# LSTM with a binary FFN on one core: x Wx computed in column tiles of 32 instead of on the whole array, and the activation tiles moved by 320 bytes

## The chip, the cores and the metric

The kernel runs on one core of one Trainium2 chip. The metric is the device time of one launch in microseconds: 328.22 us before, the median of three runs (328.02 to 329.63). A profile of one further execution shows what each engine did.

## The reference

The input x holds 32 sequences of 64 steps with 256 features. An LSTM with 256 hidden units runs over the steps and starts from `cond`; its hidden states go through an FFN of three layers whose weights are +1 or -1, given as booleans, and the result is added to x. All of it is float32.

```python
xW = x @ Wx + b                             # 32 x 64 x 1024, Wx is 256 x 1024
for t in range(64):
    a = xW[:, t] + prev_h @ Wh              # 32 x 1024
    i, f, o = sigmoid(a[:, :256]), sigmoid(a[:, 256:512]), sigmoid(a[:, 512:768])
    g = tanh(a[:, 768:])
    c = f * c + i * g
    h = o * tanh(c)
# FFN over all h: 512 (as [h, -h]) -> 1024 -> 1024 -> 256
y = s0 * ([h, -h] @ w(k0)); y = 2 * relu(y)
y = s1 * (y @ w(k1));       y = 2 * relu(y)
return x + s2 * (y @ w(k2))                 # w(k) = where(k, 1, -1)
```

## The kernel before

The 64 steps are cut into NB = 4 blocks of SB = 16. For a block of 16 steps and 32 sequences, x Wx is 512 columns wide, and so is each FFN matmul.

**x Wx** (`x_block`, L223 to L244). The 1024 outputs are cut into NM = 8 pieces of 128 rows (tile px, one PSUM bank each). Each piece is the product of 128x128 slices of Wx with the transposed x (tile xT, made by `turn_x`, L202, on VectorE), in two halves of 256 columns and with two slices of the contraction (k). The two float32 operands make every `nc.tensor.matmul` into two matmul instructions of the PE, so a piece has 4 matmuls and 8 instructions, and the kernel has 256 px instructions in all. A finished piece is moved by `finish_x` (L246): ScalarE adds the bias (tile xb, L254) and VectorE transposes it into xg (L251), where the 4 x 32 rows of the piece come to lie beside each other for the recurrence.

The order of Wx's columns in a piece isn't the order of the input. Row q*32 + j of a piece is output column q*64 + b*32 + j of the gate. So `order_wx` (L211) copies the columns of each gate g (tiles wx, wx_rest) into a tile wxo that has them in this order, two copies for each gate: the first on VectorE (L448), the others on ScalarE (L451, L459, L460).

**The recurrence.** `gates_from_h` (L284) computes h Wh of one step. The 32 sequences make the stationary side 32 columns wide, so four products with different quarters of Wh (q = 0 to 3) go to the four column tiles of 32 of the array: 8 matmuls, 16 instructions. `cell_step` (L298) adds xg on VectorE (tile `a`), takes sigmoid and tanh on ScalarE (sig, cand, th), forms kept, new, c and h on VectorE, and transposes h into hist, which the next step's gates read.

**The FFN** (`ffn_block`, L384) takes a block of h, split in two parts (hhi and hlo, made by `split_h`, L337 and L338), through the three layers: 128x128 weights, 512 columns, type float32r, one instruction for each matmul: 768 in all (L390, L419, L404).

**The order of the work.** Each engine executes its instructions in the order in which the program issues them. `x_block(0)` comes first and whole; then, for each step t, the gates of t, the cell's work, and then a share of the remaining matmuls, taken from a generator `fill()` that runs through x blocks 1 to 3 and then through the four FFN blocks. Steps 0 to 16 carry the three x blocks (10 or 12 px instructions a step, `goal`, L504), the later ones FFN matmuls (12 a step). What is left of the FFN after step 63 follows as a tail. `vector_queue` and `scalar_queue` hold the work that follows a piece until it has its turn in the step.

**The start.** Before its first real matmul, the PE multiplies zeros WARM_UP = 8 times (p_idle, L446). The loads go out on the queues of SP and ScalarE: x of block 0, Wx's gate 0, then on SP gate 1 (wx), gates 2 and 3 together (wx_rest, in a buffer of the xg pool), Wh, x of block 1, and the booleans of the FFN. A load is issued once the load eight places ahead of it has landed. During `x_block(0)` a dictionary `then` (L458) places further work after the n-th xg transposition: the order_wx of gates 2 and 3, `turn_x(1, 0)` (n = 5) and `turn_x(1, 1)` (n = 7), which make xT of block 1, and the transposition of the first h (hT, n = 6).

**Memory.** The pool const holds all weights of the recurrence and the FFN (wh, w0, w1, w2) and, behind them, small tiles, among them `warm`, of which the kernel uses two columns. The other pools, with x, xg, the activations (act), hist, hhi, hlo and the cell's tiles, follow. In this kernel the const pool ends on a multiple of 512 bytes, and so each tile of 2 KB or more in the later pools and each 128-column slice of the weights starts on such a multiple.

Of the kernel before, what the change touches and what calls it, by code (L numbers as in the profile page):

```python
# [24 lines left out]
F32 = mybir.dt.float32  # L28
# [8 lines left out]
def lstm_ffn(ctx: ExitStack, tc: tile.TileContext, x, cond, wx_d, wh_d, b_d, k0_d, k1_d, k2_d, s0_d, s1_d, s2_d, out):  # L37
    nc = tc.nc
    P = 128
    N, T, D = x.shape  # L40
    H = cond.shape[1]
    G = 4 * H
    NQ = 4
# [4 lines left out]
    NM = G // P  # L48
# [3 lines left out]
    SH = 4  # L52
    PER_STEP = 12
    LAG = SB + 1
    WARM_UP = 8

    const = ctx.enter_context(tc.tile_pool(name="const", bufs=1))
    xpool = ctx.enter_context(tc.tile_pool(name="x", bufs=4))
    gpool = ctx.enter_context(tc.tile_pool(name="xg", bufs=NB))
# [9 lines left out]
    def act(shape, dtype, name):  # L69
        return apool.tile(shape, dtype, tag="act", name=name)  # L70
# [18 lines left out]
    w1 = const.tile([P, FC0, F1], F32R, name="w1")  # L89
    w2 = const.tile([P, 2, FC1, P], F32R, name="w2")  # L90

    warm = const.tile([P, 40], F32, name="warm")
    nc.vector.memset(warm, 0.0)
    idle = const.tile([P, 512], mybir.dt.bfloat16, name="idle")
    nc.vector.memset(idle, 0.0)

    wx_rows = wx_d.rearrange("(q b j) g -> q j b g", q=NQ, b=2)
    wx_first = [act([P, 2, H], F32, f"wx_{g}") for g in range(2)]
    wx_rest = gpool.tile([P, 2, 2 * H], F32, tag="xg", name="wx_rest")
    wxf = wx_first + [wx_rest[:, :, ts(g, H)] for g in range(2)]  # L100

    def rows(t, q):
        return t[q * 32 : (q + 1) * 32]

    load_x(0, 0, [nc.sync, nc.scalar])
    for q in range(NQ):
        engine = (nc.sync, nc.scalar)[q % 2]
        engine.dma_start(out=rows(wx_first[0], q), in_=wx_rows[q, :, :, :H])
    load_x(0, 1, [nc.sync, nc.scalar])

    nc.scalar.activation(warm[:, 1:2], warm[:, :1], AF.Sigmoid)
# [1 line left out]
    b_rows = b_d.rearrange("(g q b j) -> q g b j", g=4, q=NQ, b=2)  # L113
    for q in range(NQ):
        nc.gpsimd.dma_start(out=b_raw[q * 32 : q * 32 + NM], in_=b_rows[q])
    for q in range(NQ):
        nc.sync.dma_start(out=rows(wx_first[1], q), in_=wx_rows[q, :, :, ts(1, H)])
    for q in range(NQ):
        nc.sync.dma_start(out=rows(wx_rest, q), in_=wx_rows[q, :, :, 2 * H :])
    wh_rows = wh_d.rearrange("(q b j) g -> q j b g", q=NQ, b=2)  # L120
    for q in range(NQ):
        nc.sync.dma_start(out=rows(wh, q), in_=wh_rows[q])
    h_first = const.tile([P, HQ], F32, name="h_first")
# [11 lines left out]
    for i in range(2):  # L135
        t = act([P, 2, F0], U8, f"k0_{i}")
# [63 lines left out]
    xT = {}  # L200

    def turn_x(i, half):  # L202
        full = act([P, SB // 2, 2, N], F32, f"xT{i}_{half}")
        nc.vector.transpose(
            full.rearrange("p t b n -> p (t b n)"), xq[i, half].rearrange("p t j -> p (t j)")
        )
        xT[i, half] = full

    wx = []

    def order_wx(g, copy):  # L211

        t = act([P, 2, 2, P], F32, f"wxo{g}")
        for k in range(2):
            copy(  # L215
                t[:, k].rearrange("p b (q j) -> p b q j", q=NQ),
                wxf[g][:, k, :].rearrange("p (q b j) -> p b q j", q=NQ, b=2),
            )
        wx.append(t)

    xg = {}

    def x_block(i):  # L223
        xg[i] = gpool.tile([P, SB, G // NQ], F32, tag="xg", name=f"xg{i}")
        side = 2 if i == 0 else 1
        for m0 in range(0, NM, side):
            ps = [ps_f.tile([P, 2, SB // 2, N], F32, tag="pf", name=f"px{i}_{m0 + j}") for j in range(side)]
            for half in range(2):
                for j in range(side):
                    g, b = divmod(m0 + j, 2)  # L230
                    for k in range(2):
                        nc.tensor.matmul(  # L232
                            ps[j][:, half],
                            wx[g][:, k, b, :],
                            xT[i, half][:, :, k, :],
                            start=(k == 0),
                            stop=(k == 1),
                            skip_group_check=True,
                        )
                        if k == 0:  # L240
                            yield 2
                    if half:
                        finish_x(i, m0 + j, ps[j])
                    yield 2  # L244
# [199 lines left out]
    p_idle = ps_f.tile([P, TB], F32, tag="pf", name="p_idle")  # L444
    for n in range(WARM_UP):
        nc.tensor.matmul(p_idle, idle[:, :P], idle, start=True, stop=True)  # L446
    turn_x(0, 0)
    order_wx(0, nc.vector.tensor_copy)  # L448
    turn_x(0, 1)
    nc.vector.transpose(bias, b_raw)  # L450
    order_wx(1, nc.scalar.copy)  # L451
    for i in range(4):
        load_bits(i)
    hT = const.tile([P, 2, N], F32, name="hT_first")
    c = cell.tile([P, HQ], F32, tag="c", name="c_first")
    nc.vector.memset(c, 0.0)

    then = {  # L458
        1: lambda: order_wx(2, nc.scalar.copy),  # L459
        3: lambda: order_wx(3, nc.scalar.copy),  # L460
        5: lambda: turn_x(1, 0),
        6: lambda: nc.vector.transpose(hT, h_first.rearrange("p (b j) -> p b j", b=2)),
        7: lambda: turn_x(1, 1),
    }
    n = 0
    for _ in x_block(0):
        if vector_queue:
            flush_vector()
            n += 1
            if n in then:  # L470
                then[n]()


    def fill():
        for i in range(1, NB):
            yield from x_block(i)
        for b in range(NB):
            yield from ffn_block(b)
# [14 lines left out]
    for t in range(T):  # L493
        g = gates_from_h(t, hT)
        c, hT = cell_step(t, g, c)
# [54 lines left out]
```

## Time and profile before

| what | value |
|---|---|
| median of three runs | 328.22 us (328.02 to 329.63) |
| the profiled execution | 329.2 us, span 327.4 us |
| PE busy | 316.1 us, 97% of the span |
| VectorE (DVE) busy | 175.0 us, 53% |
| ScalarE (ACT) busy | 127.5 us, 39% |
| first px matmul, first gates matmul | at 5.59 us and 21.61 us |
| steps 0 to 16 (with x Wx) | from 21.61 us to 86.70 us |
| HBM read, written | 8.16 MB, 2.10 MB |

In the rows of the page and of the trace, PE is the matmul row of TensorE, L is the line of the kernel, and `out<-in` are the program's tiles. A group's row gives its busy time in us and the mean time of one in ns, then the idle time of the engine ahead of it and what ended that. A row in order of time begins with its start and its length in us; in brackets stand the engine's idle time before it and what ended it. Matmuls overlap, so a row's length isn't its share of the PE's time; the distance from one start to the next is.

### The profile page before, as it was taken

To read this page: it belongs to the slowest core of one execution; us is meant where nothing else is said; L and a number is where in the kernel's file an instruction comes from. 1 tells how busy PE (TensorE), PEld (TensorE's weight loads), DVE (VectorE), ACT (ScalarE), POOL (GpSimd) and SP (SyncE) were. 2 spreads that over 40 slices of the span, in tenths; PEclk is the share of its full clock that TensorE was granted. 3 is DMA by queue.
4 is the path that set the end of the run, shared out by engine and by line. 5 is a ranking of instruction groups with operands and counts; after the bars stand their busy time and mean duration, and the time that the engine had idled before them with its cause. 6 is when DMAs were issued, how large, how long until landed. Compare 5 with 4: busy or idle time off the path is not lost.

```text
span 327.4 us, 5478 instructions
## 1 busy us (share of the span) xinstructions
PE 316.1 (97%) x2056; PEld 217.2 (66%) x2056; DVE 175.0 (53%) x540; ACT 127.5 (39%) x330; POOL 9.0 (3%) x27
## 2 busy tenths in 40 slices
PE   7998999999999999999999999999999999999992
PEld 3876666667666666666666666666666666888881
DVE  3357766765685445446856454568564444811114
ACT  1534576666553523233523232335332322511111
POOL 6200000000000000000000000000000000000001
PEclk9999999999999999999999999999999999999997
DMA  6956000105100000000010300000110000130002
GB/s 141 218 147 140 3 19 16 34 16 124 24 2 1 2 0 0 2 2 1 0 34 8 91 0 2 0 3 0 32 34 0 2 1 2 48 80 3 0 0 64
DMA packets 30538, 10.62 MB, mean 32 GB/s; under 512 B 27944, under 2 KB 29992, under 8 KB 30512
## 3 DMA queue, kind: packets, MB, share of 16 engines
q1 hardware_dynamic: 27904, 9.58, 12.1%
q10 hardware_dynamic: 2336, 0.66, 0.9%
q8 instruction: 16, 0.26, 0.3%
q0 software_dynamic: 272, 0.04, 0.1%
q14 instruction: 10, 0.08, 0.1%
HBM read 8.16 MB, written 2.10 MB: 31 GB/s over the span
## 4 chain that ended last, share of the span: by engine, by line
PE 81%; DVE 6%; DMA 4%; ACT 3%; SPq 3%; issue 1%; ACTq 0%; DVEq 0%
PE p L419 38%; PE gates L288 18%; PE p L390 10%; PE po L404 9%; PE px L232 7%; DMA wh<-in_L_cond_Wh_dram 2%; DVE xg L251 1%; ACT xb L254 1%; DVE a L300 1%; SPq L138 1%; DMA wx<-in_L_cond_Wx_dram 1%; DVE w L182 1%; ACT th L317 1%; DMA x<-in_x_dram 1%; DMA k<-in_L_ffn_k_dram 1%
## 5 line engine op out<-in xcount | busy, mean ns | idle before, releaser
L288 PE MATMUL gates<-wh,hist 128*32 128x256 f32 x1008 | 67.5, 385 | 2.7 <-DVE hist L324 2.7
L232 PE MATMUL px<-xT,wxo 128*128 128x256 f32 x256 | 62.1, 396 | 0.7 <-DVE wxo L215 0.7
L305 ACT ACTIVATE sig<-a 128x192 f32<-128x192 f32 x64 | 23.3, 364 | 95.8 <-DVE a L300 95.8
L232 PEld LDWEIGHTS px<-xT,wxo 128*128 128x128 f32 x256 | 48.6, 195 | 14.9 <-issue 5.8
L300 DVE TENSOR_TENSOR a<-gates,xg 128x256 f32<-128x256 f32 x64 | 27.0, 422 | 56.5 <-PE gates L288 56.3
L288 PEld LDWEIGHTS gates<-wh,hist 128*32 128x32 f32 x1008 | 26.9, 109 | 35.6 <-issue 20.2
L317 ACT ACTIVATE th<-c 128x64 f32<-128x64 f32 x64 | 16.4, 257 | 35.7 <-DVE c L315 35.4
L319 DVE TENSOR_TENSOR h<-sig,th 128x64 f32<-128x64 f32 x64 | 14.4, 225 | 24.4 <-ACT th L317 24.4
L251 DVE STREAM_TRANSPOSE xg<-xb 128x512 f32<-128x512 f32 x32 | 22.2, 695 | 9.2 <-ACT xb L254 9.2
L390 PE MATMUL p<-hhi,w 128*128 128x512 f32 x64 | 26.1, 408 | 0.0
L390 PE MATMUL p<-hlo,w 128*128 128x512 f32 x64 | 25.2, 393 | 0.0
L254 ACT ACTIVATE xb<-px,small 128x512 f32<-128x512 f32 x32 | 21.6, 675 | 4.9 <-PE px L232 4.9
L311 DVE TENSOR_TENSOR kept<-sig,c 128x64 f32<-128x64 f32 x63 | 13.2, 209 | 8.3 <-ACT sig L305 8.3
L324 DVE STREAM_TRANSPOSE hist<-h 128x64 f32<-128x64 f32 x64 | 15.7, 246 | 2.2
L390 PEld LDWEIGHTS p<-hhi,w 128*128 128x128 f32 x64 | 12.0, 187 | 6.1 <-issue 3.3
L315 DVE TENSOR_TENSOR c<-kept,new 128x64 f32<-128x64 f32 x64 | 14.4, 225 | 2.2
L307 ACT ACTIVATE cand<-a 128x64 f32<-128x64 f32 x64 | 15.4, 240 | 0.0
L313 DVE TENSOR_TENSOR new<-sig,cand 128x64 f32<-128x64 f32 x64 | 14.0, 219 | 0.0
L419 PE MATMUL p<-a_2h,w 128*128 128x512 f32 x32 | 13.9, 434 | 0.0
L390 PEld LDWEIGHTS p<-hlo,w 128*128 128x128 f32 x64 | 12.0, 188 | 2.4
L419 PE MATMUL p<-a_6h,w 128*128 128x512 f32 x32 | 13.5, 423 | 0.0
L419 PE MATMUL p<-a_4h,w 128*128 128x512 f32 x32 | 13.2, 414 | 0.0
(122 smaller groups left out, 487.7 us busy)
## 6 DMA issues: line engine op xcount, KB each, us to landing
x<-in_x_dram SPq DMA_DIRECT2D x60, 64.0 KB, 2.3
out_dram<-o SPq DMA_DIRECT2D x28, 64.0 KB, 1.8
bits<-in_L_ffn_k_dram SPq DMA_DIRECT2D x10, 128.0 KB, 2.3
wh<-in_L_cond_Wh_dram SPq DMA_DIRECT2D x4, 256.0 KB, 6.4
wx_rest<-in_L_cond_Wx_dram SPq DMA_DIRECT2D x4, 128.0 KB, 3.3
k<-in_L_ffn_k_dram SPq DMA_DIRECT2D x8, 64.0 KB, 1.9
wx<-in_L_cond_Wx_dram SPq DMA_DIRECT2D x6, 64.0 KB, 2.8
x<-in_x_dram ACTq DMA_DIRECT2D x4, 64.0 KB, 2.6
```

Source lines behind the costliest of these rows:

```text
L232: nc.tensor.matmul(ps[j][:, half], wx[g][:, k, b, :], xT[i, half][:, :, k, :], start=(k == 0), stop=(k == 1), skip_group_check=True,)
L251: nc.vector.transpose(out_t[:, :, ts(m, 32)], tmp.rearrange("p (t n) -> p t n", n=N))
L254: nc.scalar.activation(tmp, p.rearrange("p h t n -> p (h t n)"), AF.Identity, bias=bias[:, m : m + 1])
L288: nc.tensor.matmul(g[q * N : (q + 1) * N], hT[:, k, :], wh_q[:, k, q], start=(k == 0), stop=(k == 1), skip_group_check=True,)
L300: nc.vector.tensor_tensor(a.rearrange("p g j -> p (g j)"), g.rearrange("p g j -> p (g j)"), xg[t // SB][:, t % SB, :], ALU.add)
L305: nc.scalar.activation(sig, a[:, 0:3, :], AF.Sigmoid)
L307: nc.scalar.activation(cand, a[:, 3, :], AF.Tanh)
L317: nc.scalar.activation(th, c, AF.Tanh)
L324: nc.vector.transpose(hT, h.rearrange("p (b j) -> p b j", b=2))
L390: nc.tensor.matmul(p, w0[:, k, ts(m, P)], a[:, k, :], start=(n == 0), stop=(n == 3))
L404: nc.tensor.matmul(po[m], w2[:, m, k], a1[k][n], start=(k == 0 and n == 0), stop=(k == FC1 - 1 and n == 1))
L419: nc.tensor.matmul(p1[m], w1[:, k, ts(m, P)], a0[k][n], start=(k == 0 and n == 0), stop=(k == FC0 - 1 and n == 1),)
```

## The change

x Wx is computed in the tiling of the gates. Each matmul of 128 stationary columns becomes four of 32 columns (q = 0 to 3), which write the four partition quarters of the same px tile and read the same xT. They take their columns straight from the loaded Wx (slice `ts(2 * q + b, 32)`), so the ordered copies and `order_wx` are gone. Wx is loaded as four tiles of the act pool, one for each gate, with 16 loads in place of 12. In x block 0 only the first two pieces are computed side by side, the others one by one; before, all were computed in pairs. The PE multiplies zeros 9 times rather than 8. `turn_x(1, 0)`, hT and `turn_x(1, 1)` come after the 4th, 5th and 6th xg transposition instead of the 5th, 6th and 7th. The tile `warm` grows by 80 columns, 320 bytes, so that x, xg, the activations, hist, hhi, hlo and the cell's tiles start 320 bytes farther on; the weights in the const pool keep their places.

```diff
-    WARM_UP = 8
+    WARM_UP = 9
...
-    warm = const.tile([P, 40], F32, name="warm")
+    warm = const.tile([P, 40 + 80], F32, name="warm")
...
-    wx_first = [act([P, 2, H], F32, f"wx_{g}") for g in range(2)]
-    wx_rest = gpool.tile([P, 2, 2 * H], F32, tag="xg", name="wx_rest")
-    wxf = wx_first + [wx_rest[:, :, ts(g, H)] for g in range(2)]
+    wx = [act([P, 2, H], F32, f"wx{g}") for g in range(4)]
...
-    for q in range(NQ):
-        nc.sync.dma_start(out=rows(wx_first[1], q), in_=wx_rows[q, :, :, ts(1, H)])
-    for q in range(NQ):
-        nc.sync.dma_start(out=rows(wx_rest, q), in_=wx_rows[q, :, :, 2 * H :])
+    for g in range(1, 4):
+        for q in range(NQ):
+            nc.sync.dma_start(out=rows(wx[g], q), in_=wx_rows[q, :, :, ts(g, H)])
...
-    def order_wx(g, copy):
-
-        t = act([P, 2, 2, P], F32, f"wxo{g}")
-        for k in range(2):
-            copy(
-                t[:, k].rearrange("p b (q j) -> p b q j", q=NQ),
-                wxf[g][:, k, :].rearrange("p (q b j) -> p b q j", q=NQ, b=2),
-            )
-        wx.append(t)
...
-        side = 2 if i == 0 else 1
-        for m0 in range(0, NM, side):
+        for m0, side in ((0, 2), *((m, 1) for m in range(2, NM))) if i == 0 else ((m, 1) for m in range(NM)):
...
                     for k in range(2):
-                        nc.tensor.matmul(
-                            ps[j][:, half],
-                            wx[g][:, k, b, :],
-                            xT[i, half][:, :, k, :],
-                            start=(k == 0),
-                            stop=(k == 1),
-                            skip_group_check=True,
-                        )
+                        for q in range(NQ):
+                            nc.tensor.matmul(
+                                ps[j][q * 32 : (q + 1) * 32, half],
+                                wx[g][:, k, ts(2 * q + b, 32)],
+                                xT[i, half][:, :, k, :],
+                                start=(k == 0),
+                                stop=(k == 1),
+                                skip_group_check=True,
+                            )
                         if k == 0:
                             yield 2
...
     turn_x(0, 0)
-    order_wx(0, nc.vector.tensor_copy)
     turn_x(0, 1)
     nc.vector.transpose(bias, b_raw)
-    order_wx(1, nc.scalar.copy)
...
     then = {
-        1: lambda: order_wx(2, nc.scalar.copy),
-        3: lambda: order_wx(3, nc.scalar.copy),
-        5: lambda: turn_x(1, 0),
-        6: lambda: nc.vector.transpose(hT, h_first.rearrange("p (b j) -> p b j", b=2)),
-        7: lambda: turn_x(1, 1),
+        4: lambda: turn_x(1, 0),
+        5: lambda: nc.vector.transpose(hT, h_first.rearrange("p (b j) -> p b j", b=2)),
+        6: lambda: turn_x(1, 1),
     }
```

More of the change, by code (lines that the diff above doesn't have):

```diff
@@ L107, in lstm_ffn @@
         engine = (nc.sync, nc.scalar)[q % 2]
-        engine.dma_start(out=rows(wx_first[0], q), in_=wx_rows[q, :, :, :H])
+        engine.dma_start(out=rows(wx[0], q), in_=wx_rows[q, :, :, :H])
     load_x(0, 1, [nc.sync, nc.scalar])
@@ L207, in turn_x @@
         xT[i, half] = full
-    wx = []
-    def order_wx(g, copy):
-        t = act([P, 2, 2, P], F32, f"wxo{g}")
-        for k in range(2):
-            copy(
-                t[:, k].rearrange("p b (q j) -> p b q j", q=NQ),
-                wxf[g][:, k, :].rearrange("p (q b j) -> p b q j", q=NQ, b=2),
-            )
-        wx.append(t)
     xg = {}
```

## The prediction

> **What bounds the kernel now.** I read the page's costliest groups first, then the PE's instructions in order of time in three stretches, then the PE's waits. The groups:
>
> ```profile
> L288 PE MATMUL gates<-wh,hist 128*32 128x256 f32 x1008 | 67.5, 385 | 2.7 <-DVE hist L324 2.7
> L232 PE MATMUL px<-xT,wxo 128*128 128x256 f32 x256 | 62.1, 396 | 0.7 <-DVE wxo L215 0.7
> L390 PE MATMUL p<-hhi,w 128*128 128x512 f32 x64 | 26.1, 408 | 0.0
> ```
>
> Gates run in tiles of 128x32, four of them side by side; x Wx and the FFN use the whole 128x128 array. The PE waits only 3.4 us for anything in these rows, so it is the bound, but the means (385 ns) are not its rate, because matmuls overlap. The rate is in the distances between starts. First, steps 5 to 8 (steps 0 to 16 carry x Wx):
>
> ```profile
> 41.18 1.07 PE L288 MATMUL gates<-wh,hist 128*32 128x256 f32 x16 [0.37 <-DVE hist L324]
> 42.18 2.86 PE L232 MATMUL px<-xT,wxo 128*128 128x256 f32 x12
> 44.97 1.07 PE L288 MATMUL gates<-wh,hist 128*32 128x256 f32 x16
> 45.97 2.86 PE L232 MATMUL px<-xT,wxo 128*128 128x256 f32 x12
> 48.76 1.07 PE L288 MATMUL gates<-wh,hist 128*32 128x256 f32 x16
> 49.76 2.42 PE L232 MATMUL px<-xT,wxo 128*128 128x256 f32 x10
> 52.47 1.07 PE L288 MATMUL gates<-wh,hist 128*32 128x256 f32 x16 [0.29 <-DVE hist L324]
> ```
>
> A step of 12 px matmuls takes 3.79 us, and no wait ends inside it: PE-bound. A step of 10 ends with an idle PE until the transposed h is there: 3.71 us, set by the recurrence. Taken singly in the trace, px starts are 215.8 ns apart and four gates matmuls share one such slot (starts 7 ns apart). But px to gates is 309 ns, the last gates matmul to the first px 309, first px to second 320. Of the 3788 ns, 16 slots are 3453 ns; 335 are lost around the two changes of tiling.
>
> From step 17 the FFN fills the steps, 12 matmuls each, 3.99 us a step with about 0.26 us to spare over the recurrence:
>
> ```profile
> 103.65 0.50 PE L419 MATMUL p<-a_2h,w 128*128 128x512 f32 x1
> 103.99 0.40 PE L419 MATMUL p<-a_2l,w 128*128 128x512 f32 x1
> 104.23 0.40 PE L419 MATMUL p<-a_3h,w 128*128 128x512 f32 x1
> 104.46 0.40 PE L419 MATMUL p<-a_3l,w 128*128 128x512 f32 x1
> ...
> 292.64 0.39 PE L419 MATMUL p<-a_1l,w 128*128 128x512 f32 x1
> 292.87 0.39 PE L419 MATMUL p<-a_2h,w 128*128 128x512 f32 x1
> ```
>
> After the first, each is 224 to 240 ns behind the one before (mean 231), in the same order in nearly every step; in the tail without gates it is 226.7. The px matmuls stay at 215.8. So something delays the 512-column matmuls by 11 to 24 ns each, 768 times. All their moving tiles and all weight slices start at multiples of 512 bytes. Last, the start:
>
> ```profile
> 1.28 3.59 PE L446 MATMUL p_idle<-idle 128*128 128x512 bf16 x8 [1.28 <-DVE idle L95]
> 5.24 0.62 DVE L215 COPY wxo<-wx 128x256 f32<-128x256 f32 x2 [0.65 <-DMA wx<-in_L_cond_Wx_dram]
> 5.59 16.09 PE L232 MATMUL px<-xT,wxo 128*128 128x256 f32 x64 [0.72 <-DVE wxo L215]
> 9.30 0.71 ACT L215 COPY wxo<-wx 128x256 f32<-128x256 f32 x2 [3.75 <-DMA wx<-in_L_cond_Wx_dram]
> 18.76 0.67 DVE L204 STREAM_TRANSPOSE xT<-x 128x512 f32<-128x512 f32 x1
> 22.21 0.67 DVE L204 STREAM_TRANSPOSE xT<-x 128x512 f32<-128x512 f32 x1
> 23.58 0.42 DVE L300 TENSOR_TENSOR a<-gates,xg 128x256 f32<-128x256 f32 x1
> ```
>
> p_idle stops about 0.7 us before px. The px starts are 427 ns apart until 9.6 us and 216 from 9.9 on.
>
> **What the Trainium skill says.** "TensorEngine Tiling (Array Packing)", Key Properties: "Changing tiling mode (not just tile) drains the TensorE"; the 309 and 320 ns agree. "TensorE: Matmul & The Clock Gate", Part 1: the PE runs at half clock until a free-running window of about 3.4 us was busy; the step from 427 to 216 ns agrees, and so does its lateness after the pause. The same page, Back-to-back issue gap: columns/2.4 + 2.5 ns, 215.8 for 512; the FFN's 231 does not reach it. "SBUF — State Buffer", Who interferes with whom: PE has two independent read ports, for moving operand and weights. By that, addresses shouldn't matter; the unexplained 11 to 24 ns leave it open.
>
> **Part by part.** The sums are against the profiled execution (329.2 us, span 327.4, so 1.8 around it).
>
> *Start.* The four order_wx, eight copies (DVE 0.62 us a pair, ACT 0.71), go. The first px waits for its DMA alone (5.23 us, where the copy began) instead of 5.59, and a ninth p_idle (427 ns) closes the pause. If that makes the half-rate end by about 6.5 us, the 16 slots of g=0 take 2.4 at 427 and 13.6 at 216: done near 9.25. The second block's weights landed at 9.2 and need no copy, so px_2 starts near 9.3 rather than 11.16, and 48 slots later (10.36 us) gates begin near 19.7 instead of 21.6. But VectorE is late: turn_x(1,0) now stands after xg_3, ready at 14.4, while its four loads landed at 17.0 to 17.5, behind the 1 MB of wh. SP issues four more loads ahead of wh, 0.47 us each: 1.9 us. I cost these at nothing, since SP already waited between 10.5 and 16.8 us for earlier loads to land, and the bytes ahead are the same; without that cover up to 1.9 us. So DVE runs turn (17.5), xg_4, hT, xg_5, turn, xg_6, xg_7 back to back, 0.62 each and 0.2 for hT, and step 0's `a` starts near 21.65: 1.93 us earlier. hT at 19.0 is in time for gates. If the half-rate ends at 9.7 as before, px_2 starts at 10.9, gates at 21.3, xg_7 ends at 23.0: 0.56 earlier. The median is 1.0 below the profiled execution; an end of the half-rate near 6.3 would have brought px_2 to 10.08 there (the copy ends at 10.0), 1.08 us earlier. I read the median as such a run: against it the start gains 0.85.
>
> *Steps 1 to 16.* x Wx becomes 1024 matmul instructions instead of 256, four to a slot: the same slots, if they share it as gates do (16 in 863 ns). Same tiling, so most of the 335 ns go, on the PE. But the step is then set by h: hist's end plus 147 ns. Adding those per step gives 60.24 us against 60.76 now: 0.52. Step 12 (4.03 us, `a` 0.33 late because xb, hhi and hlo follow a late px) should lose part of that, as px ends 0.2 to 0.3 earlier in its step; I take 0.3. Sum 0.8. The rest of the 335 ns becomes idle PE, about 0.25 us a step. This also covers px slots up to some 236 ns long.
>
> *The 320 bytes.* The warm tile's 320 more bytes put every activation tile 320 bytes past a multiple of 512; weights stay. No row of before shows another offset. Bound below: all 768 matmuls at 215.8 instead of 230.9, 11.6 us gained. Above: all at 240, the slowest spacing seen, 7.0 us lost. The middle, 228, gains 2.3 us; since no change at all is as possible, I take half, 1.1 us (229.5 ns).
>
> Sum: 329.2 - 1.93 - 0.8 - 1.1 = 325.4; from the median, 328.2 - 0.85 - 0.8 - 1.1 = 325.5. I forecast 325.4.
>
> **Rivals.** (1) *Slower: the offset makes weight loads and moving reads clash more.* Place: the FFN steps and the tail, where the PE has no slack. Price: 0.768 us per ns of spacing. It decides from 4.3 ns on (3.3 us, the 1.7 of the other parts and 1.6 to the bound). For it: the spacing moves from 224 to 240 by small shifts of time alone. Against: the tail at 226.7 isn't near a best case, and the skill's two ports. At 236 ns: 326.5 + 3.9 = 330.4.
> (2) *The offset removes much of the delay.* For it: 32-column and 128-column px with half the reading rate show none, so it looks like reads in each other's way; at present all start alike. At 221 ns: 326.5 - 7.6 = 318.9.
> (3) *The change doesn't do what it says at the start.* The loads of x block 1 land 1 to 2 us later, VectorE stands in turn_x(1,0), hT behind it holds the gates, and the early px gain nothing: 328.2 - 0.8 + 0.4 = 327.8, pad idle.
> (4) *px slots longer than 216 ns in the new tiling,* as four streams read one xT tile where gates read four places of wh. At 240 ns: 64 slots of block 0, 1.5 us, and 4 ns over cover in the steps: about 327.
>
> **How the numbers follow.** Forecast (pad between -5 and +2 ns): 0.50, own range 322.5 to 328. Rival 2: 0.22. Rival 1: 0.16. Rivals 3 and 4: 0.12. The low end cuts half of rival 2 (319), the high end about half of rival 1 (330). A measurement tells some 0.5% (1.64 us) from no change: bounds 326.6 and 329.9. Faster: 0.22, and 0.44 of the forecast: 0.66. Slower: 0.14, nearly all of rival 1. Same: 0.20, rivals 3 and 4 and the forecast's upper end.
>
> **What would show it.** In the profile after: gates and px starts 216 ns apart across the change, no 309 or 320; every step of 0 to 16 near 3.71 us with "DVE hist" ending the PE's idle time, together about 4 us; px from 5.3 us, px_2 near 9.3, the first `a` near 21.7 after a VectorE wait for x; hhi and a matmuls with new spacings, mean 229.5. Wrong, if FFN spacings fall under 225 or exceed 235, if the half-rate lasts to 9.7, or if px slots exceed 236 ns.

## The result and the profile after

The changed kernel takes 329.81 us (median of 15 runs, 328.86 to 330.31), the kernel before 328.29 us in the same rounds (15 runs, 327.78 to 329.89). The ratio is 1.0029, with a 95% interval of 1.0015 to 1.0043: slower by about 0.3%, within the 0.5% that was called no change. It is an estimate from all the runs, here and below, and not the quotient of the two medians (1.0046). I had forecast 325.4 us.

The times of the kernel before lie in two groups, near 328.2 and near 329.5 us, and its profiled execution (329.2 us, span 327.4) is of the upper one; so spans differ by less than medians do. A median of that kernel also says how many of its runs fell into each group.

The changed kernel's profiled execution took 329.64 us, its span is 327.87 us, 0.45 more than before. Its costliest matmul groups:

```profile
L275 PE MATMUL gates<-wh,hist 128*32 128x256 f32 x1008 | 67.5, 384 | 6.0 <-DVE hist L311 5.6
L219 PE MATMUL px<-xT,wx 128*32 128x256 f32 x1024 | 59.2, 379 | 1.9 <-DVE xT L202 1.2
```

There are 1024 px instructions instead of 256 and their busy time is less, so four of them do share a slot. The PE's wait for the transposed h has doubled, 2.7 to 5.6 us, and px has a wait of its own for xT. In the PE's instructions in order of time, steps 10 to 13:

```profile
60.85 1.07 PE L275 MATMUL gates<-wh,hist 128*32 128x256 f32 x16 [0.48 <-DVE hist L311]
61.71 2.80 PE L219 MATMUL px<-xT,wx 128*32 128x256 f32 x48
64.56 1.07 PE L275 MATMUL gates<-wh,hist 128*32 128x256 f32 x16
65.42 2.80 PE L219 MATMUL px<-xT,wx 128*32 128x256 f32 x48
68.27 1.07 PE L275 MATMUL gates<-wh,hist 128*32 128x256 f32 x16
69.13 2.37 PE L219 MATMUL px<-xT,wx 128*32 128x256 f32 x40
72.21 1.07 PE L275 MATMUL gates<-wh,hist 128*32 128x256 f32 x16 [0.71 <-DVE hist L311]
```

Gates to px is now 0.86 us, four slots of 216 ns, where it was 1.00. A step with 12 of the old matmuls is 3.71 us (60.85 to 64.56) instead of 3.79, as long as steps 7, 9 and 15 with 10 of them: h sets it. Step 12, also with 10, takes 3.94 (68.27 to 72.21), since its `a` starts 1.37 us after its gates instead of 1.13. The FFN beside the steps, and in the tail:

```profile
104.27 0.40 PE L406 MATMUL p<-a_2l,w 128*128 128x512 f32 x1
104.50 0.40 PE L406 MATMUL p<-a_3h,w 128*128 128x512 f32 x1
...
292.14 0.39 PE L406 MATMUL p<-a_1h,w 128*128 128x512 f32 x1
292.37 0.39 PE L406 MATMUL p<-a_1l,w 128*128 128x512 f32 x1
```

Singly, starts are 225 to 237 ns apart beside the steps (mean 230.6 over 460 distances) and 229.1 in the tail (211 distances), where the kernel before had 224 to 240 (mean 232.7) and 227.2 (226.7 in the prediction). So the spacings have changed, one down and the other up; the first experiments show that the 320 bytes do it. Last, the start, SP's queue included. Two rows of the kernel before:

```profile
8.17 1.83 SPq L122 DMA_DIRECT2D wh<-in_L_cond_Wh_dram  x4
10.05 7.11 SPq L79 DMA_DIRECT2D x<-in_x_dram  x8
```

and the changed kernel:

```profile
5.92 1.93 PE L219 MATMUL px<-xT,wx 128*32 128x256 f32 x32 [0.69 <-DMA wx<-in_L_cond_Wx_dram]
8.28 0.71 DVE L202 STREAM_TRANSPOSE xT<-x 128x512 f32<-128x512 f32 x1 [3.10 <-DMA x<-in_x_dram]
9.05 12.29 PE L219 MATMUL px<-xT,wx 128*32 128x256 f32 x224 [1.20 <-DVE xT L202]
10.81 2.63 SPq L120 DMA_DIRECT2D wh<-in_L_cond_Wh_dram  x4
13.48 5.29 SPq L80 DMA_DIRECT2D x<-in_x_dram  x8
19.89 0.71 DVE L202 STREAM_TRANSPOSE xT<-x 128x512 f32<-128x512 f32 x1 [3.95 <-DMA x<-in_x_dram]
21.11 0.20 DVE L445 STREAM_TRANSPOSE hT_first<-h_first 128x64 f32<-128x64 f32 x1
21.37 1.07 PE L275 MATMUL gates<-wh,hT_first 128*32 128x256 f32 x16
21.87 0.71 DVE L202 STREAM_TRANSPOSE xT<-x 128x512 f32<-128x512 f32 x1
23.87 0.42 DVE L287 TENSOR_TENSOR a<-gates,xg 128x256 f32<-128x256 f32 x1
```

px runs at the full rate from its first matmul, as hoped, but it stops at 7.4 us for the second half of xT. VectorE stands 3.95 us in turn_x(1, 0), until 19.89, with hT, the second turn and four transpositions into xg behind it. The gates lose some 0.2 us by this, as px itself lasts until 21.3; the first `a`, which needs all of these transpositions, starts at 23.87 us; before, at 23.58. In the chain of work that ended last, followed back from there:

```profile
13.01 5.44 DMA wh<-in_L_cond_Wh_dram
18.46 3.29 DMA x<-in_x_dram
21.87 0.71 DVE xT L202
```

The last load of x block 1 is issued when the last of wh has landed, and lands at 21.75 us, just ahead of turn_x(1, 1). px alone would not have held `a` so long: its last piece has passed ScalarE (xb) at 22.10 us, and where nothing else is late `a` starts 0.84 us after that (so in the fastest kernel below): some 22.9 us, an estimate from the two traces.

The spans, stage by stage (us; starts of the first gates matmul of a step where not said otherwise):

| stage | before | after | difference | forecast |
|---|---|---|---|---|
| start to the first `a` | 23.58 | 23.87 | +0.29 | -1.93 |
| first `a` to gates of step 1 | 2.36 | 2.37 | +0.01 | |
| steps 1 to 16 | 60.76 | 60.81 | +0.05 | -0.8 |
| steps 17 to 62 | 183.39 | 182.63 | -0.76 | -1.1 for this row and the next two |
| step 63 and the FFN's tail, to the last matmul | 50.78 | 51.16 | +0.38 | |
| last matmul to the end | 6.55 | 7.03 | +0.48 | |
| sum | 327.42 | 327.87 | +0.45 | -3.8 |

### The profile page after: what moved, and what is told of

Read it like the earlier page. It is cut to its first block, busy times and chain, and to the rows that moved or that the text cites. A ratio compares the mean times of both kernels' runs of the same rounds, so it can differ in the third digit from the quotient of the medians.

```text
span 327.9 us, 7012 instructions
## 1 busy us (share of the span) xinstructions
PE 311.5 (95%) x2825; PEld 207.6 (63%) x2825; DVE 174.6 (53%) x538; ACT 125.6 (38%) x324; POOL 9.1 (3%) x27
## 4 chain that ended last, share of the span: by engine, by line
PE 79%; DVE 7%; DMA 6%; ACT 3%; SPq 2%; issue 2%; ACTq 0%; DVEq 0%
PE p L406 38%; PE gates L275 18%; PE p L377 10%; PE po L391 9%; PE px L219 5%; DMA x<-in_x_dram 4%; DVE xg L238 2%; DMA wh<-in_L_cond_Wh_dram 2%; DVE a L287 1%; ACT xb L241 1%; ACT th L304 1%; DVE xT L202 1%; SPq L117 1%; DVE h L306 1%; SPq L120 1%
## 5 line engine op out<-in xcount | busy, mean ns | idle before, releaser
L219 PE MATMUL px<-xT,wx 128*32 128x256 f32 x1024 | 59.2, 379 | 1.9 <-DVE xT L202 1.2
L275 PEld LDWEIGHTS gates<-wh,hist 128*32 128x32 f32 x1008 | 27.6, 109 | 40.3 <-issue 22.2
L219 PEld LDWEIGHTS px<-xT,wx 128*32 128x32 f32 x1024 | 37.9, 110 | 19.9 <-DVE xT L202 3.1
L241 ACT ACTIVATE xb<-px,small 128x512 f32<-128x512 f32 x32 | 21.6, 675 | 10.6 <-PE px L219 10.5
```

The source lines that it names most:

```text
L219: nc.tensor.matmul(ps[j][q * 32 : (q + 1) * 32, half], wx[g][:, k, ts(2 * q + b, 32)], xT[i, half][:, :, k, :], start=(k == 0), stop=(k == 1),
L241: nc.scalar.activation(tmp, p.rearrange("p h t n -> p (h t n)"), AF.Identity, bias=bias[:, m : m + 1])
L275: nc.tensor.matmul(g[q * N : (q + 1) * N], hT[:, k, :], wh_q[:, k, q], start=(k == 0), stop=(k == 1), skip_group_check=True,)
```

## The experiments

In all of them the whole computation is done. The kernel before ran beside each; its medians in the rounds that follow were 329.10, 329.31, 328.27, 328.58 and 328.26 us. They shift with the shares of the two groups, so a kernel's ratio is to its own rounds, and part of a difference between ratios of different rounds can be a difference of these medians.

### The 320 bytes

Taken out of the changed kernel:

```diff
-    warm = const.tile([P, 40 + 80], F32, name="warm")
+    warm = const.tile([P, 40], F32, name="warm")
```

> The changed kernel with the warm tile at 40 columns again, so that the activation tiles start at multiples of 512 bytes. Theory S (the start lost the gain: four more loads ahead of Wh and of x block 1, VectorE standing in turn_x(1,0) with hT behind it): within 0.3% of the changed kernel, first gates again near 21.4 us, VectorE again about 4 us in front of turn_x(1,0); FFN spacings back to 240, 235, 233, 236, 224 in a step (mean 232.7) and 226.7 in the tail, which costs 0.8 us in the steps and gives 0.5 back in the tail. Rival P (the 320 bytes slow the loads into the moved tiles, or the matmuls): the loads of x block 0 land by 6.5 us and those of x block 1 by 17.5 us again, and the time falls by 1 us or more.

329.29 us (14 runs, 328.66 to 330.32), ratio 1.0012 (0.9995 to 1.0030). Steps 17 to 62 are back at 183.31 us, step 63 and tail at 50.77, last matmul to end at 6.32. The loads of x block 1 land as late as in the changed kernel (19.1 to 21.8 us), so the offset isn't what makes them late.

Put into the kernel before (the same edit the other way round):

> The kernel before with the 320 bytes alone. Theory S: the FFN spacings become those of the changed kernel (two patterns in turn, about 231 in a step, 229 in the tail), 0.8 us less in the steps and 0.5 us more in the tail: 0.1% faster or no difference; loads land as in the kernel before. Rival P: slower by about 1 us (0.3%), as much as the whole change.

329.71 us (14 runs, 328.31 to 331.36), ratio 1.0014 (0.9994 to 1.0033). Steps 17 to 62 take 182.60 us, step 63 and tail 51.16, last matmul to end 7.29: the three differences of the table again (the last one larger), without the new tiling. Where does the last one come from? All DMA in the stretch from 321 us (packets, MB and share of the 16 DMA engines for each queue; then the stores, with KB of each and the median us from issue to landing), before:

```profile
q1 hardware_dynamic: 1088, 0.26, 15.4%
q10 hardware_dynamic: 1088, 0.26, 14.7%
...
out_dram<-o SPq DMA_DIRECT2D x4, 64.0 KB, 1.8
out_dram<-o ACTq DMA_DIRECT2D x4, 64.0 KB, 2.1
```

and after:

```profile
q10 hardware_dynamic: 1088, 0.26, 18.1%
q1 hardware_dynamic: 1088, 0.26, 16.2%
...
out_dram<-o SPq DMA_DIRECT2D x4, 64.0 KB, 2.5
out_dram<-o ACTq DMA_DIRECT2D x4, 64.0 KB, 2.6
```

The same packets and bytes take a larger share of the DMA engines, and the last stores take 0.5 to 0.7 us longer from issue to landing. Singly, the 2048 packets of 256 bytes take 19.3 ns instead of 16.8. The Trainium skill offers a reason, in "DMA: Bandwidth & Descriptors", How a descriptor splits into AXI transactions: a descriptor that doesn't start on a multiple of 256 bytes begins its first transaction at the boundary below and pays for the bytes before its start. With 64 bytes over a multiple, a packet of 256 bytes fetches 320: an estimate of 25% more from that page, where the trace has 15%. No run tries another offset, so this reason isn't shown. No step of the prediction has the stores.

The price was measured once more, in a kernel whose times scatter less, the fastest one below (under ScalarE's late sigmoid) but with the 80 columns:

> The kernel with four loads, x block 2 earlier, the turns reordered and the six copies on ScalarE, with the 80 columns put in. Theory (the 80 columns gain 0.7 us in the FFN beside the steps and lose 0.4 in the FFN alone and 0.5 at the last stores): steps 17 to 63 at 182.6 us instead of 183.4, from the last matmul to the end 6.9 to 7.1 instead of 6.5, span 325.5 to 326.0, median 327.4 to 327.9 beside 327.4 without. Rival (the columns cost what the changed kernel lost): median 328.3 or more. Third (they gain): median below 327.0.

328.07 us (22 runs, 327.77 to 328.54), ratio 0.9981 (0.9969 to 0.9993), beside 327.42 us (13 runs, 327.06 to 328.02), ratio 0.9965 (0.9951 to 0.9979), without them; the medians of before were 328.26 and 328.27. Steps 17 to 62 go from 183.37 to 182.64 us, step 63 and tail from 50.74 to 51.16, last matmul to end from 6.54 to 7.06: together +0.21. The same three parts sum to +0.33 when the offset is put into the kernel before, and to +0.42 in the changed kernel against the run without it. So the gain is a little more than cancelled; the medians put the offset at +0.65 here and +0.52 in the changed kernel. Where the medians' other 0.1 to 0.4 us lie isn't settled: the start differs from one execution to the next by as much.

### The places of the turns

The three steps of VectorE one transposition later, as in the kernel before:

```diff
-        4: lambda: turn_x(1, 0),
-        5: lambda: nc.vector.transpose(hT, ...),
-        6: lambda: turn_x(1, 1),
+        5: lambda: turn_x(1, 0),
+        6: lambda: nc.vector.transpose(hT, ...),
+        7: lambda: turn_x(1, 1),
```

> The changed kernel with turn_x(1,0), hT and turn_x(1,1) at n = 5, 6 and 7 as in the kernel before. Theory S: hT still stands behind turn_x(1,0), so the first gates start as in the changed kernel, but one xg transposition fewer is left after it: the first a some 0.6 us earlier, the time 0.4 to 0.6 us lower. Rival P: no difference beyond 0.2 us.

329.74 us (22 runs, 328.95 to 330.60), ratio 1.0021 (1.0006 to 1.0035). x block 1 lands at 19.5 to 21.9 us, the first `a` starts at 23.90: no difference. The places only say where VectorE waits for the same load.

So hT went ahead of the wait, and the second turn behind the first `a`:

```diff
-        4: lambda: turn_x(1, 0),
-        5: lambda: nc.vector.transpose(hT, ...),
-        6: lambda: turn_x(1, 1),
+        3: lambda: nc.vector.transpose(hT, ...),
+        7: lambda: turn_x(1, 0),
+        8: lambda: on_vector(lambda: turn_x(1, 1)),
```

> The changed kernel with hT after the 3rd xg transposition, turn_x(1,0) after the 7th and turn_x(1,1) after the first a, so that no load of x block 1 stands ahead of hT. Theory S: gates follow px without a pause, near 20.5 to 21.1 us, the first a 1 us or more earlier than in the changed kernel (23.9), the time 1 us lower, 328.8 or less. Rival P: 0.3 us at most.

329.73 us (22 runs, 328.86 to 331.26), ratio 1.0022 (1.0009 to 1.0036). The first gates come at 20.69 instead of 21.37 us and the first `a` at 22.48 instead of 23.87, and all of it is gone by step 3. VectorE in step 2, in order of time:

```profile
30.74 0.71 DVE L202 STREAM_TRANSPOSE xT<-x 128x512 f32<-128x512 f32 x1 [1.46 <-DMA x<-in_x_dram]
31.37 0.71 DVE L180 SCALAR_TENSOR_TENSOR w<-k,nsgn,w0t 128x512 fp32r<-128x512 uint8 x1
32.00 0.42 DVE L287 TENSOR_TENSOR a<-gates,xg 128x256 f32<-128x256 f32 x1
```

This turn is of x block 2, and its load is as late as those before it on SP. VectorE waits 1.46 us, and `a` starts 2.58 us after its gates instead of 1.20: step 2 takes 5.15 us. In the changed kernel the same wait is 0.40 us and step 2 takes 4.09. Fewer waits at the first load, more at the next: a chain of loads in one queue is the bound. The loads of x block 2 then went ahead of the bits (the FFN's booleans):

```diff
+    for half in range(2):
+        load_x(2, half, [nc.sync])
     for i in range(4):
         load_bits(i)
...
-    for i in (2, 3):
-        for half in range(2):
-            load_x(i, half, [nc.sync])
+    for half in range(2):
+        load_x(3, half, [nc.sync])
```

> The kernel of the run with hT early and the turns of block 1 late, and with the loads of x block 2 issued ahead of those of the first four rows of booleans. Theory S (the loads of x bound the start: what hT early gained was lost to the wait of turn_x(2,0) in step 2): the a of step 2 starts 1.2 us after its gates instead of 2.58, the x phase ends 1 us earlier or more, the time is 1 us below that run's 329.7. Rival (the start is not bound by x's loads): step 2 late again, within 0.3 us.

328.28 us (22 runs, 327.93 to 329.37), ratio 0.9981 (0.9970 to 0.9992), 1.45 us less than the kernel it was made from, though their ratios belong to different rounds. In step 2:

```profile
28.74 0.71 DVE L202 STREAM_TRANSPOSE xT<-x 128x512 f32<-128x512 f32 x1
29.39 0.75 DVE L180 SCALAR_TENSOR_TENSOR w<-k,nsgn,w0t 128x512 fp32r<-128x512 uint8 x1
30.06 0.42 DVE L287 TENSOR_TENSOR a<-gates,xg 128x256 f32<-128x256 f32 x1
```

No wait is left, and step 2 takes 3.78 us.

### The number of loads

In the changed kernel SP issues the first load of wh at 10.81 us instead of 8.17, and the first of x block 1 at 13.48 instead of 10.05. Four issues of 0.47 us are 1.9 of the 2.64 us; the rest is a first issue of gate 1 that comes 0.4 us later and a wait for x block 0. To have fewer loads without a new buffer, I first made them of 128 partitions, six for gates 1 to 3 instead of twelve:

```diff
-        for q in range(NQ):
-            nc.sync.dma_start(out=rows(wx[g], q), in_=wx_rows[q, :, :, ts(g, H)])
+        for b in range(2):
+            nc.sync.dma_start(out=wx[g][:, b], in_=wx_rows[:, :, b, ts(g, H)])
```

> The changed kernel with the gates 1 to 3 of Wx in six loads of 128 KB over all 128 partitions instead of twelve of 64 KB over 32. Theory S (the four more loads ahead of Wh and x push all later loads back): the loads of x block 1 land by 18 us instead of 18.7 to 21.7, VectorE stands 2 us less in turn_x(1,0), no wait of turn_x(2,0) in step 2, the x phase 1 us shorter, the time near 328.7. Rival (the bytes alone set the landing, or their destination): x block 1 lands after 19 us again, within 0.3 us of the changed kernel.

335.74 us (5 runs, 334.94 to 335.95), ratio 1.0198 (1.0172 to 1.0224). This tells nothing of the number, since the loads themselves are slow (from 9.0 to 12.4 us the DMA engines are busy for 27% of the time, in the changed kernel from 6 to 14 us for 71%): PE stops four times for wx and has the whole weights of gates 1, 2 and 3 at 12.42, 16.91 and 21.22 us, where the twelve loads had all landed by 14.0.

Next the tiling alone: the kernel before with its four loads for gates 2 and 3, its order_wx, its pad and turns, and only the matmul split.

```diff
-                        nc.tensor.matmul(
-                            ps[j][:, half],
-                            wx[g][:, k, b, :],
...
+                        for q in range(NQ):
+                            nc.tensor.matmul(
+                                ps[j][q * 32 : (q + 1) * 32, half],
+                                wx[g][:, k, b, q * 32 : (q + 1) * 32],
```

> The kernel before with the column tiling of x Wx alone: the ordered copies, the loads, the 320 bytes, WARM_UP and the order of VectorE stay as before. Theory S: px slots of 216 ns, no drain at the change to gates and back, steps 0 to 16 set by the recurrence near 3.71 us, gates 1 to gates 17 in 60.1 us or less instead of 60.76, the time 0.5 us lower in runs of the same kind. Rival (the column tiling itself costs: longer slots, or the delayed sigmoid of step 6 comes with it): 60.7 us or more, no gain.

328.62 us (22 runs, 327.08 to 329.26), ratio 0.9980 (0.9966 to 0.9994). Here steps 1 to 16 take 60.17 us; I had worked out 60.24 from the recurrence, and less with step 12. And this kernel with its four loads of 128 KB cut into eight of 64 KB, nothing else:

```diff
-        nc.sync.dma_start(out=rows(wx_rest, q), in_=wx_rows[q, :, :, 2 * H :])
+        nc.sync.dma_start(out=rows(wx_rest, q)[:, :, :H], in_=wx_rows[q, :, :, ts(2, H)])
+    for q in range(NQ):
+        nc.sync.dma_start(out=rows(wx_rest, q)[:, :, H:], in_=wx_rows[q, :, :, ts(3, H)])
```

> The tiling alone, with the kernel before's buffers and copies, and its four loads of gates 2 and 3 (128 KB each) split into eight of 64 KB. Theory (each load more on SP's queue puts back what stands behind it by 0.47 us): weights of gates 2 and 3 land by 13.8 us instead of 11.8, x block 1 by 21.5 instead of 19.5, VectorE stands at the turn of its first half until then with the transpose of h behind it, first gates at 21.2 to 21.5 instead of 20.1, first a at 23.4 to 23.7 instead of 22.2, and the profiled execution 1.0 to 1.5 us over that of the tiling alone (327.2). Rival (the number of loads is not it; the buffers that the copies free early, or the copies themselves, keep the loads on time): x block 1 lands by 19.5, first a at 22.2, time within 0.3 us of the tiling alone.

329.13 us (19 runs, 328.24 to 329.66), ratio 1.0020 (1.0008 to 1.0032): the same bytes in four more loads turn 0.2% faster into 0.2% slower. By the times themselves it is less, 0.5 us between the medians (328.62 and 329.13); the kernel before had more of its slower group in the rounds of the first. The start of the tiling alone, in order of time:

```profile
8.61 1.83 SPq L122 DMA_DIRECT2D wh<-in_L_cond_Wh_dram  x4
10.49 6.60 SPq L79 DMA_DIRECT2D x<-in_x_dram  x8
17.71 0.71 DVE L204 STREAM_TRANSPOSE xT<-x 128x512 f32<-128x512 f32 x1 [0.25 <-DMA x<-in_x_dram]
22.20 0.43 DVE L301 TENSOR_TENSOR a<-gates,xg 128x256 f32<-128x256 f32 x1
```

and with eight loads:

```profile
10.87 1.85 SPq L124 DMA_DIRECT2D wh<-in_L_cond_Wh_dram  x4
12.77 7.79 SPq L79 DMA_DIRECT2D x<-in_x_dram  x8
20.86 0.71 DVE L206 STREAM_TRANSPOSE xT<-x 128x512 f32<-128x512 f32 x1 [1.61 <-DMA x<-in_x_dram]
24.22 0.42 DVE L303 TENSOR_TENSOR a<-gates,xg 128x256 f32<-128x256 f32 x1
```

SP reaches wh 2.26 us later, and the turn of x block 1 waits 1.61 us for its load instead of 0.25 and starts 3.15 us later. That the first `a` starts 2.02 us later doesn't show what the loads cost, though: in this execution px stay at the half rate until 9.7 us, in that of the tiling alone they run at 216 ns from their first at 5.92, and so they end 1.78 us later (22.05 instead of 20.27), which alone would account for most of it. What px doesn't touch is steps 1 to 16: 60.80 us instead of 60.17, with `a` late in steps 2 and 5. The times tell more than the two traces: the lowest went from 327.08 to 328.24 us, the highest from 329.26 to 329.66. So the four loads more cost this kernel some 0.4 to 1.2 us.

Last, the changed kernel with this one thing undone, offset, turns and p_idle left as changed. The buffer can't be that of the xg pool any more, since x blocks 1 to 3 read wx themselves; it is put in const, and act has two tiles fewer.

```diff
-    wx = [act([P, 2, H], F32, f"wx{g}") for g in range(4)]
+    wx = [act([P, 2, H], F32, f"wx{g}") for g in range(2)]
+    wx_rest = const.tile([P, 2, 2 * H], F32, name="wx_rest")
+    wx += [wx_rest[:, :, ts(g, H)] for g in range(2)]
...
-    for g in range(1, 4):
-        for q in range(NQ):
-            nc.sync.dma_start(out=rows(wx[g], q), in_=wx_rows[q, :, :, ts(g, H)])
+    for q in range(NQ):
+        nc.sync.dma_start(out=rows(wx[1], q), in_=wx_rows[q, :, :, ts(1, H)])
+    for q in range(NQ):
+        nc.sync.dma_start(out=rows(wx_rest, q), in_=wx_rows[q, :, :, 2 * H :])
```

> The changed kernel with one thing undone: the weights of gates 2 and 3 in one buffer and four loads of 128 KB, as in the kernel before; the columns, the turns' places and the 9th p_idle stay as changed. Theory (the four loads more took the gain at the start, the 80 columns net nothing): x block 1 lands by 19.7 instead of 21.7, the idle time ahead of turn_x(1, 0) falls from 3.95 to at most 2.1 us, first gates at 19.9 to 20.2 instead of 21.37, first a at 21.8 to 22.3 instead of 23.87, step 2 within 3.85 us, gates of step 17 at 84.8 to 85.2, steps 17 to 63 182.6, span 325.4 to 326.2, median 327.3 to 328.1 and ratio 0.996 to 0.999. Rival (the start is late for another reason than the number of loads): first a at 23.5 or later, span 327.5 or more, ratio 1.001 to 1.004.

```profile
18.06 0.71 DVE L205 STREAM_TRANSPOSE xT<-x 128x512 f32<-128x512 f32 x1 [3.02 <-DMA x<-in_x_dram]
22.20 0.42 DVE L290 TENSOR_TENSOR a<-gates,xg 128x256 f32<-128x256 f32 x1
```

By its trace the theory holds. In the profiled execution (327.79 us, span 326.0) VectorE's idle time ahead of turn_x(1, 0) is 3.02 us instead of 3.95, still more than the 2.1 I expected. The turn starts at 18.06 instead of 19.89, the first gates come at 20.27 and the first `a` at 22.20, 1.67 us earlier than in the changed kernel; step 2 takes 3.81 us. px ends earlier here too (20.45 instead of 21.34), as the second half of x block 0 landed at 7.20 us instead of 8.09. A cleaner pair is the run without the 320 bytes: there, with eight loads for gates 2 and 3, px ends at 20.54, and still the turn starts at 19.93 and the first `a` at 23.96. But the median is 328.92 us (14 runs, 327.79 to 330.67), ratio 1.0016 (0.9996 to 1.0036): which is what the rival expected. The profiled execution is the fastest of the 14, so something else is late in most of them.

### Why most executions don't reach it

The kernel just told, once more, for the trace of another execution:

> The kernel with four loads for gates 2 and 3 once more, for the trace of another execution. If it takes 328.5 to 329.5: by theory A step 2 is over 4.3 us and first a at 22.2; by theory B the first a comes at 23.0 or later and step 2 is below 3.9 us; by a third (the first matmuls stay at the half rate) the matmuls of px_0 and px_1 are 427 ns apart until 9.7 or later and the last of block 0 ends at 21 or later.

328.33 us, a single run. The first `a` is in time, 22.05 us, but in step 2:

```profile
28.94 0.71 DVE L205 STREAM_TRANSPOSE xT<-x 128x512 f32<-128x512 f32 x1 [0.81 <-DMA x<-in_x_dram]
29.57 0.71 DVE L183 SCALAR_TENSOR_TENSOR w<-k,nsgn,w0t 128x512 fp32r<-128x512 uint8 x1
30.20 0.42 DVE L290 TENSOR_TENSOR a<-gates,xg 128x256 f32<-128x256 f32 x1
```

Step 2 takes 4.49 us instead of 3.81, the same wait for x block 2 as above. With the loads of x block 2 ahead of the bits (the edit already shown):

> The kernel with four loads for gates 2 and 3, and the loads of x block 2 ahead of those of the bits. Theory A (in most executions the loads of x block 2 land too late for VectorE in step 2): the spread goes, median 327.6 to 328.3 and within 0.5 us of the lowest. Theory B (the first half of x block 1 lands late and holds the transpose of h behind its turn): median stays at 328.7 to 329.1, 1 us or more over the lowest.

328.16 us (22 runs, 327.85 to 329.17), ratio 0.9990 (0.9978 to 1.0002); the median is 0.3 us above the lowest instead of 1.1. In its profiled execution (328.49 us) step 2 takes 3.78 us, but the first `a` comes only at 22.98: the loads were later in it, the second half of x block 0 landing at 7.88 us and the first of x block 1 at 18.79, where the one at 327.79 us had 7.20 and 17.94. With the turns reordered instead:

> The kernel with four loads for gates 2 and 3, the transpose of h ahead of the turns of x block 1 and the second of these behind the first a. Theory B (the transpose of h stands behind a load): the spread goes, median 327.6 to 328.3 and within 0.5 us of the lowest. Theory A (x block 2 is late in step 2): median stays at 328.7 to 329.1 or rises, since what is gained ahead of the first gates is lost in step 2.

328.64 us (14 runs, 328.21 to 329.99), ratio 0.9999 (0.9984 to 1.0015). The spread shrinks here too, but the lowest time rises, so this decides less. The late x block 2 holds at least part of the 1.1 us. In all traces of this document the second half of x block 0 lands between 6.45 and 8.09 us, and that scatter isn't explained.

### ScalarE's late sigmoid

In the changed kernel and in every kernel made from it without the six copies below, the sigmoids of steps 6 and 23 start 0.3 us late. Step 6 takes 4.02 us instead of 3.71; step 23 has FFN matmuls that cover most of it. The sigmoid of step 6, from ScalarE's instructions in order of time:

```profile
47.54 0.36 ACT L292 ACTIVATE sig<-a 128x192 f32<-128x192 f32 x1 [0.93 <-DVE a L287]
```

It starts 0.83 us after its `a` starts, elsewhere 0.52. In each of these kernels the two are ScalarE's 43rd and 135th instruction in the profile, at whatever time they come, and neither is late in a kernel with order_wx, whose six copies on ScalarE stand ahead. That points to a position in the stream of instructions, not to work. Two kernels tell. The first has four loads for gates 2 and 3, no offset, x block 2 earlier and the turns reordered:

> The changed kernel with gates 2 and 3 in one buffer and four loads as in the kernel before, the 80 columns taken back, the loads of x block 2 ahead of the bits, and the transpose of h ahead of the turns of x block 1. Theory (the column tiling pays once the loads and the turns are on time; the offset nets nothing): x block 1 lands by 19.5, first gates at 19.8 to 20.1, first a at 21.7 to 22.0, step 2 at 3.71 us, steps 6 and 23 still 0.3 us long, gates of step 17 at 84.4 to 84.9, steps 17 to 63 183.3 us, span 325.0 to 325.6, median 326.5 to 327.3, ratio 0.993 to 0.997. Rival (the loads stay late for another reason): first a at 22.5 or later, span 326 or more.

327.73 us (18 runs, 327.18 to 328.69), ratio 0.9971 (0.9958 to 0.9984); first `a` at 21.56 us, span 325.65; the two sigmoids are still late, and step 6 takes 4.02 us. The second has six tiny copies in addition:

```diff
     nc.scalar.activation(warm[:, 1:2], warm[:, :1], AF.Sigmoid)
+    for j in range(6):
+        nc.scalar.copy(warm[:, 2 + j : 3 + j], warm[:, :1])
```

> The kernel of the eight loads with six one-column copies on ScalarE right after its first sigmoid; their outputs are read by nothing. Theory (the late sigmoid of steps 6 and 23 comes from where ScalarE's instructions change over to the next fetched stretch, 6 instructions nearer the start than where the order_wx copies had put it): steps 6 and 23 return to 3.71 us, or the 0.3 us moves to another place, as in the kernel before; span 0.3 to 0.6 us under that of the eight loads without the copies. Rival (the delay belongs to the work of those steps, not to the position in the instruction stream): steps 6 and 23 stay at 4.0 us, span within 0.2 us.

327.42 us (13 runs, 327.06 to 328.02), ratio 0.9965 (0.9951 to 0.9979). No sigmoid is late any more; that of step 6:

```profile
45.38 0.36 ACT L297 ACTIVATE sig<-a 128x192 f32<-128x192 f32 x1 [0.62 <-DVE a L292]
```

Step 6 takes 3.71 us. So it is what stands ahead of the sigmoid in ScalarE's stream, not the work of the step. The count alone doesn't make an instruction late: with the copies the 43rd is the sigmoid of step 5, and it is in time. That the late ones stand where ScalarE goes over to a newly fetched stretch of its instructions is a guess: a transfer of 8192 bytes on the queue that the profile calls instruction begins at 48.20 us in the changed kernel, just after the late sigmoid, and moves from 46.42 to 42.96 us with the six copies.

This is the fastest version I have, 0.35% below the kernel before.

### The ninth p_idle

The kernel before with WARM_UP = 9:

> The kernel before with nine multiplications of zeros instead of eight. Theory H (the two groups of times of the kernel before, near 328.1 and 329.6, are runs in which the half-rate of the PE ends early or late, and the ninth one makes it end early more often): fewer runs near 329.6, the median 0.5 us lower or more, and in the profile px starts 216 ns apart before 9 us. Rival (the groups come from the speed of the loads): the same two groups in the same shares.

328.07 us (22 runs, 327.73 to 329.76), ratio 0.9981 (0.9967 to 0.9996). 16 of 22 times are in the lower group, of the kernel before in these rounds only 18 of 59. Its profiled execution (329.76 us) is one of the upper group, and there px stays 427 ns apart until 10.1 us. So the ninth p_idle makes the lower group likelier, and it doesn't ensure an early end of the half-rate. The other traces of kernels with order_wx agree: the four with px at 427 ns until 9.6 to 10.2 us took 329.2 to 330.1 us, and the one with px at 216 ns from the first, of the tiling alone, took 327.19. That the two groups of the kernel before are this, and nothing else, isn't shown, since no execution of its lower group was traced.

## Why the prediction was wrong

**The four loads costed at nothing: the step that failed.** I wrote of SP's four more loads ahead of wh: "I cost these at nothing, since SP already waited between 10.5 and 16.8 us for earlier loads to land", with up to 1.9 us if that cover was gone. The wait was no cover, because what ended it stands behind the added issues itself. SP waits there, with the loads of x block 1, for those of wx_rest and wh to land. wh was issued from 8.17 us before and from 10.81 after, so it landed at 15.3 to 18.4 us instead of 13.6 to 16.8, the wait ended later, and x block 1 landed at 18.7 to 21.7 us instead of 17.0 to 18.7. turn_x(1, 0) started at 19.89, where I had 17.5, and the first `a` came at 23.87 us, not at 21.65: 0.29 later than before, where I had forecast 1.93 earlier. My rival 3 described this (the loads 1 to 2 us later, VectorE standing in turn_x(1, 0), hT behind it); I gave it and the rival with px 0.12 together, and its 327.8 us was 2 us too low. The return to four loads shows it: first `a` at 22.20, 22.05 and 22.98 us in the three traces with hT behind the first turn, against 23.87, 23.96 and 23.90 in the three with eight loads. The split of loads alone agrees, with 0.4 to 1.2 us.

**What I left out: x block 2.** The path after the first `a` has one more load in the same queue. Of a queue that is put back by 2 us I followed two loads, not the third. It costs 0.31 us in the profiled execution of the changed kernel (step 2 at 4.09 us instead of 3.78) and up to 1.4 where the start is earlier, and it scatters.

**Half-rate and copies: right in this execution.** order_wx's copies went, the half-rate ended before px began at 5.92 us, px ran at 216 ns. With the turns later, the same start kept px at 427 ns until 9.7 us in the traced execution. And px_0 and px_1 also need the second half of x block 0, which landed at 8.1 us; I had the PE running through. So px_2 began at 10.80 us instead of 9.3, and even with x block 1 in time the first `a` would have come near 22.9 rather than 21.65. That only the first two pieces of block 0 are computed side by side wasn't tried on its own.

**Steps 1 to 16: right in mechanism.** The tiling alone takes 60.17 us for what I put at 60.24. "TensorEngine Tiling (Array Packing)", Key Properties, is borne out: without the change of tiling, the 309 and 320 ns are gone. With step 12 I had put the gain at 0.8 us; it is 0.59. Step 12 went from 4.03 to 3.94 us where I took 0.3 off. In the changed kernel x block 2 in step 2 (+0.31) and the late sigmoid in step 6 (+0.31) took the gain back.

**The 320 bytes: wrong in sign.** I took half of a middle, 1.1 us gained. Measured: 0.76 gained beside the steps, 0.38 lost in the tail, 0.48 lost at the last stores, which no step of the prediction spoke of. Rivals 1 (330.4 us) and 2 (318.9 us) are both wrong, and that rival 1's time is the nearest of all to the 329.81 measured is luck: the spacing moved by -2.1 ns beside the steps and +1.9 in the tail, against +5 in the first and -10 in the second.

## What to carry to other kernels

A load costs its issue even when the bytes are no more: count the issues (0.47 us each on SP here) ahead of every load that something waits for, down the whole queue, and take a wait of the queue as cover only if what ends it doesn't itself stand behind the added issues. When a wait at one load is moved, look for the next load in that queue before booking the gain. A shift of addresses is a change to every DMA that touches these tiles too, the final stores first.

## What the runs showed of the hardware

- Spacings of 128x512 float32r matmuls depend on where the moving tiles start: with multiples of 512 bytes a series of 240, 235, 233, 236, 224, 231 ns and so on within a step, the same in nearly every step; with 320 more, two series that alternate from step to step (235, 233, 236, 229 and 231, 237, 232, 231 at their beginnings). "SBUF — State Buffer", Who interferes with whom, has PE never waiting for another engine and its two read ports independent, and so gives no reason for this; what these matmuls wait for isn't shown.
- Packets of 256 bytes from SBUF, in the last stores, took 16.8 ns from a multiple of 512 bytes and 19.3 from 320 past it.
- The weights of gate 3 were there at 21.2 us with six loads of 128 KB over 128 partitions, and at 14.0 with twelve of 64 KB over 32 partitions; the DMA engines were 27% busy during a part of the first and 71% during the second. What makes the six slow wasn't tried.
- Two sigmoids, ScalarE's 43rd instruction and its 135th, started 0.3 us late in each of ten kernels, and no sigmoid was late in the kernels where six more instructions stood ahead.
